# Keys, values and queries as seven half products in a chained PSUM bank, with the residual sums and xn kept in DRAM meanwhile, and the edge table's halves added by GpSimd

## The chip, the cores and the metric

The kernel runs on one core of one Trainium2 chip. The metric is device time in microseconds, the median of the runs; lower is better.

## The reference, cut to what matters

One graph transformer layer over 1250 nodes of 768 features, in float32: a two-layer graph attention (GNN) on 21,250 edges, a linear-attention mixer with an MLP, and a mixture of two of four experts.

```python
xn = layernorm(x)
x  = x + gnn(xn, edges) + mix(xn)
x  = x + ffn(layernorm(x))

# mix(xn)
h = layernorm(xn, ln1_w, ln1_b)
q, k, v = split(h @ qkv_w + qkv_b)            # 768 columns each, 12 heads of 64
q, k = elu(q) + 1, elu(k) + 1
kv = einsum('bhsd,bhse->bhde', k, v)
z  = 1 / einsum('bhsd,bhd->bhs', q, k.sum(-2))
y  = einsum('bhde,bhsd,bhs->bhse', kv, q, z) @ proj_w + proj_b
x1 = xn + y
out = x1 + gelu(layernorm(x1, ln2_w, ln2_b) @ fc1_w + fc1_b) @ fc2_w + fc2_b

# gnn: two attention layers; softmax over the edges into each node
e = leaky_relu(s_src[src] + s_dst[dst]); alpha = softmax of e over the edges of dst
out = segment_sum(alpha * h[src], dst) + bias   # then concat([x, out2]) @ Wu + bu
```

## The kernel before

All matrices lie in SBUF by 128 rows of features or by ten tiles of 125 nodes. Three large tiles last through the kernel: `slot_a` and `slot_x`, each 128 x 7680, and `fT`, the current normalized activations turned (six blocks of 128 features x 1250 nodes). `acc` and `xn` are views of `slot_a` and `slot_x` by ten node tiles: the sum of the residual branches, and the mixer's stream. PSUM has eight banks: two of the pool `p_tp` (`bank4`) and six of the pool `p_mm` (`bank`, one tag, rotating).

The kernel is written with a tile framework. It tracks which tile is read and written, puts in all waits, and orders each engine's instructions at compile time from a list in program order; an instruction that is ready can be placed ahead of earlier ones that are not. Instructions wrapped in `pin` keep program order among themselves on their engine. A tile pool that is closed gives its space to the next one opened at that place.

The stages, in program order:

1. Lines 407 to 509: x is loaded and normalized; `xn` is turned into `fT`; `acc` gets `xn @ Wu` (ps_u). In between, `edge_piece` (line 274) turns the edge list into places in a table of 1250 x 1250 edge multiplicities in DRAM, and GpSimd scatters 170 columns of 125 edges into it, each with an indirect DMA that adds (line 301), alternately into two tables `tabs[0]` and `tabs[1]`, the two halves.
2. Lines 512 to 551: for each of ten tiles, the GNN's first features (ps_g), stored to DRAM from `gt`, a tile of the pool `pk`; `fT` takes the ln1 values meanwhile (`norms`).
3. Lines 564 to 646, in the pool `kvp`: for each tile, keys (ps_k), values (ps_v) and their product (ps_kv). `keys_tile` also adds a bias row `arow` to `acc` and stores it to DRAM (`acc_d`), and adds the projection's bias to `xn`. `wk`, `wv`, `wq`, `wp` are whole weight matrices, loaded on SP's queue.
4. Lines 678 to 720, in the pool `qp`: queries (ps_q) in three column groups of 4, 3 and 3 tiles (`SPLITS`), written to `qT` in `slot_a`. After each group, `ps_z` gets the normalizer and DVE takes its reciprocal and multiplies. `project` (line 688) multiplies kv into the projection's weights ahead of the last group's divisions.
5. Lines 725 to 767: the output projection (ps_p) into `xn`, statistics, and for each tile the ln2 values, turned through PSUM (ps_t) into `fT`.
6. Lines 774 to 1166: the MLP in twelve groups of 256 hidden columns, each in two node ranges (`MIX`). `fc1_unit` (line 781) already computes its product as seven half products: `differences` and `combined` (lines 93 and 103) form sums of quarters of the activations and of the weights, and `product` (line 115) multiplies them, with `more=True` adding onto a bank that a copy has been taken from. `hpool` holds its copies `c1` and `u2`.
   The GNN's attention (`gnn`, line 989) is a generator that yields a cost in us for each step; `spend` (line 1117) adds the cost of each piece of MLP work to a credit, which starts at -20, and takes as many GNN steps as the credit pays for. First of these is `largest` (line 870): for each of ten row blocks the table block is fetched and DVE takes, over four heads, the largest score into each node. Before the fetch, `merged` (line 863) adds the second table to the first in DRAM with an accumulating DMA.
7. Lines 1167 to the end: router, two experts, last layer norm.

## Time and profile before

| | |
|---|---|
| median of 3 runs | 1934.47 us (1929.26 to 1935.96) |
| the profiled execution | 1930.96 us, its span 1929.2 us |
| granted TensorE clock | 0.996 |
| TensorE, DVE, ACT, GpSimd busy | 1896.4, 1330.9, 790.0, 500.7 us |
| scatters into the edge table (line 301) | 170, from 60.4 to 577 us |
| keys and values | 208 to 379 us |
| queries | 377 to 465 us; last divisions to 490 us |
| output projection | 476 to 560 us |
| MLP with the GNN beside it | 560 to 1365 us |
| experts | from 1375 us |

Rows of the trace give start and duration in us, the engine, the line of the kernel, the operation, output `<-` inputs, the shape and how many instructions are merged; in square brackets stands the idle time ahead and what ended it. A float32 matmul of the program is two instructions of the trace. L78 is the line of a helper.

### The profile page before, as it was taken

What the parts mean: (1) busy time and instruction counts of PE and PEld (TensorE: products, weight loads), DVE (VectorE), ACT (ScalarE), POOL (GpSimd) and SP (SyncE); (2) the same over time, 40 slices, a digit from 0 to 9 for tenths busy, and PEclk for the clock granted to TensorE, in tenths of its full rate; (3) what the DMA queues carried; (4) which work ended last, traced back from release to release, by engine and by line L of the source; (5) the groups of instructions that cost most, each with busy time, mean ns of one, the idle gap of its engine ahead of it and who ended that gap; (6) DMA issues with size and microseconds to landing.
All of it is one profiled execution on the core that took longest, in us unless ns stands there. A gap on an engine that the chain in (4) does not pass through costs nothing.

```text
span 1929.2 us, 19359 instructions
## 1 busy us (share of the span) xinstructions
PE 1896.4 (98%) x6978; PEld 1245.5 (65%) x6978; DVE 1330.9 (69%) x2307; ACT 790.0 (41%) x1170; POOL 500.7 (26%) x340
## 2 busy tenths in 40 slices
PE   8989999999999999999999999999999999999998
PEld 7555566545566667877877655666766666666664
DVE  3889533356556976676766967865777777777778
ACT  3223211113131118677874166764374343534330
POOL 2166577688872120111110111100041000000000
PEclk9999999999999999999999999999999999999999
DMA  9844622311119742232442532301485301010023
GB/s 339 272 130 99 198 25 21 69 5 2 2 6 184 142 130 66 74 95 73 113 108 72 142 106 72 104 8 44 129 97 85 85 1 66 0 66 27 31 81 112
DMA packets 180663, 167.78 MB, mean 87 GB/s; under 512 B 108929, under 2 KB 152481, under 8 KB 179287
## 3 DMA queue, kind: packets, MB, share of 16 engines
q0 software_dynamic: 126608, 68.01, 20.4%
q1 hardware_dynamic: 53760, 98.46, 16.0%
q8 instruction: 55, 0.90, 0.2%
q14 instruction: 42, 0.34, 0.1%
q10 hardware_dynamic: 198, 0.07, 0.0%
HBM read 133.94 MB, written 38.20 MB: 89 GB/s over the span
## 4 chain that ended last, share of the span: by engine, by line
PE 70%; issue 9%; POOL 8%; DVE 6%; DMA 5%; ACT 1%; POOLq 0%; DVEq 0%
PE ps_f L830 14%; PE ps_p L78 13%; PE ps_r L78 12%; POOL tab L301 8%; PE ps_o L1006 7%; PE ps_a L119 7%; PE ps_c L119 3%; PE ps_f L1406 3%; PE ps_o L1045 2%; PE ps_k L593 2%; PE ps_v L614 2%; PE ps_d L119 2%; DMA tab<-mult,place_e 1%; PE ps_u L1058 1%; PE ps_g L521 1%
## 5 line engine op out<-in xcount | busy, mean ns | idle before, releaser
L301 POOL DMA_INDIRECT tab<-mult,place_e x170 | 355.0, 2088 | 166.1 <-DMA tab<-mult,place_e 117.5
L830 PE MATMUL ps_f<-w,v 128*125 128x384 f32 x960 | 338.8, 487 | 1.7 <-DVE slot_x L835 1.7
L830 PEld LDWEIGHTS ps_f<-w,v 128*125 128x125 f32 x960 | 177.8, 188 | 110.1 <-issue 11.1
L835 DVE TENSOR_TENSOR slot_x<-ps_f,slot_x 125x384 f32<-125x384 f32 x240 | 131.5, 555 | 56.8 <-PE ps_f L830 52.9
L961 DVE TENSOR_TENSOR wt<-ee 125x375 f32<-125x375 f32 (+1 forms) x180 | 105.9, 590 | 89.7 <-PE ps_o L1006 57.7
L1006 PEld LDWEIGHTS ps_o<-turns,wt 125*125 125x125 f32 x800 | 136.2, 187 | 27.6 <-DVE wt L962 2.2
L1006 PE MATMUL ps_o<-turns,wt 125*125 125x193 f32 x800 | 149.9, 327 | 1.6 <-DVE wt L962 1.6
L956 ACT ACTIVATE ee<-bt,s 125x375 f32<-125x375 f32 (+1 forms) x180 | 114.8, 638 | 88.9 <-DVE wt L961 79.4
L78 PE MATMUL ps_p<-fT,w 128*128 128x312 f32 (+1 forms) x432 | 125.5, 426 | 0.6 <-ACT c L1324 0.6
L962 DVE SCALAR_TENSOR_TENSOR wt<-wt,slot_a 125x375 f32<-125x375 f32 (+1 forms) x180 | 106.0, 591 | 4.9 <-DVE rd L1063 0.2
L78 PEld LDWEIGHTS ps_p<-fT,w 128*128 128x128 f32 x432 | 81.5, 189 | 36.4 <-ACT c L1324 1.1
L78 PE MATMUL ps_r<-w,slot_x 128*125 128x384 f32 x260 | 94.5, 486 | 0.0
L521 PE MATMUL ps_g<-fx,zT 128*125 128x388 f32 x240 | 81.9, 498 | 4.1 <-DVE zT L330 4.1
L119 PE MATMUL ps_a<-fT,w 128*128 128x250 f32 (+1 forms) x288 | 85.0, 426 | 0.7 <-DVE slot_x L736 0.7
L1368 DVE SCALAR_TENSOR_TENSOR slot_a<-ps_r,gate,slot_a 125x384 f32<-125x384 f32 x100 | 60.7, 615 | 33.3 <-PE ps_r L78 33.0
L78 PE MATMUL ps_p<-xt,ws 128*128 128x313 f32 (+1 forms) x288 | 83.5, 425 | 0.0
L495 PE MATMUL ps_u<-wu,fT 128*125 128x384 f32 x240 | 80.0, 490 | 2.4 <-ACT fT L491 2.4
L593 PE MATMUL ps_k<-wk,fT 128*125 128x384 f32 x240 | 80.2, 486 | 0.0
L898 DVE SCALAR_TENSOR_TENSOR slot_a<-turns,s,slot_a 125x1250 f32<-125x1250 f32 x54 | 79.6, 1516 | 0.2
L614 PE MATMUL ps_v<-wv,fT 128*125 128x384 f32 x240 | 79.2, 486 | 0.0
L731 PE MATMUL ps_p<-wq,slot_a 128*125 128x384 f32 x240 | 78.7, 486 | 0.0
L703 PE MATMUL ps_q<-fT,wq 128*128 128x375 f32 (+1 forms) x216 | 76.4, 512 | 0.0
(335 smaller groups left out, 3356.5 us busy)
## 6 DMA issues: line engine op xcount, KB each, us to landing
turns<-g_d POOLq DMA_DIRECT2D x12, 942.4 KB, 13.8
w<-in_L_mix_fc_w_dram SPq DMA_DIRECT2D x12, 768.0 KB
w<-in_L_mix_fc_w_dram SPq DMA_DIRECT2D x24, 384.0 KB
slot_a<-tab POOLq DMA_DIRECT2D x14, 610.4 KB, 6.5
w<-in_L_ffn_w_dram SPq DMA_DIRECT2D x11, 768.0 KB
w<-in_L_ffn_w_dram SPq DMA_DIRECT2D x5, 1536.0 KB
slot_a<-tab POOLq DMA_DIRECT2D x40, 183.1 KB, 3.2
kr<-key_d SPq DMA_DIRECT2D x6, 1062.5 KB
```

The source lines that it names most:

```text
L78: return lambda *args, **kw: pin(getattr(self.engine, name)(*args, **kw))
L119: engine.matmul(ps, wt[:, k, :], x[:, k, :], start=k == 0 and not more, stop=k == n - 1, skip_group_check=more,)
L301: nc.gpsimd.indirect_dma_start(out=tabs[c % 2][:, :], out_offset=bass.IndirectOffsetOnAxis(ap=place[:, c : c + 1], axis=0), in_=mult[:, c ...
L521: nc.tensor.matmul(ps[:TP, :388], zT[:, k, :], fx[:, k, h2 * 388 : (h2 + 1) * 388], start=k == 0, stop=k == KC - 1,)
L593: nc.tensor.matmul(ps[:TP, :w], fT[:, k, tc_], wk[:, k, c0 : c0 + w], start=k == 0, stop=k == KC - 1,)
L614: nc.tensor.matmul(ps[:TP, :w], fT[:, k, tc_], wv[:, k, c0 : c0 + w], start=k == 0, stop=k == KC - 1,)
L830: nc.tensor.matmul(ps, v_of[c][:, f, h, at : at + TP], lasts[g, j][:, f, :], start=f == 0, stop=f == 1,)
L835: nc.vector.tensor_tensor(o, ps, o, ALU.add)
L956: nc.scalar.activation(e[:, 0, :w], bt[:TP, 0, :w], AF.Exp, bias=s[:, 0, h, c : c + 1])
L961: nc.vector.tensor_tensor(wt[:, :w], e[:, 0, :w], e[:, 1, :w], ALU.max)
L962: nc.vector.scalar_tensor_tensor(wt[:, :w], wt[:, :w], 1.0, adj, op0=ALU.min, op1=ALU.mult)
L1006: nc.tensor.matmul(sums[i // 2][:TP, (i % 2) * 193 : (i % 2 + 1) * 193], wt[:, i * TP : (i + 1) * TP], gh[:, c, :], start=c == 0 and i % 2 ...
```

## The change

- Keys and values are computed for pairs of tiles (t, t + 5) by seven products of 3 matmuls each instead of four times 6; queries for six parts (two node ranges, three pairs of column blocks) in the same way. `seven_weights` forms the weight sums, `by_tokens` the activation differences into `xt`, now also a part of `slot_a`. Every chain of a pair uses three banks: `pa`, `pd`, `pc`. Two parts overlap by two products (`overlapped`).
- `acc` is stored whole to `acc_d` on ACT's queue during stage 2 and not added to `arow`; the row goes to DRAM (`brow_d`) and comes in as a row of the GNN's last weights (`wu2x`). `xn` plus the projection's bias is stored to `xn_d` (`leave`), the keys take its place in `slot_x` (`kk`), then the queries (`qT`); it is loaded back into `slot_a` ahead of the output projection. So `acc` and `xn` change places.
- The value bias is added when kv is formed, from the sums of the keys.
- The projection's bias is loaded into the pool `kvp`; `wp` is loaded in `qp`, `hpool` is opened only after `qp` is closed; the pool of `wq` and `wsum` is opened at t == 8 of stage 2.
- The divisions of the first node range stand between query parts, those of the second (12) behind `project`. The output projection takes tiles in the order 0 1 5 6, 2 3 7, 4 8 9.
- `largest` loads both tables' blocks, GpSimd adds them and stores the sum; two buffers take the place of three. The pace is 4.5 for 5.0 and the first credit -27 for -20.

```diff
...
-    qT = slot_a[:, : KC * N].rearrange("p (k n) -> p k n", n=N)
+    qT = slot_x[:, : KC * N].rearrange("p (k n) -> p k n", n=N)
...
+    def seven_weights(w, to):
+        return combined(
+            nc.vector, *(w[:, k : k + 3, c : c + 384] for c in (0, 384) for k in (0, 3)), to
+        )
+    xt = slot_a[:, 2 * D : 2 * D + 9 * HALF].rearrange("p (a b n) -> p a b n", a=3, b=3)
...
+        if t == 1:
+            nc.scalar.dma_start(rows(acc_d, TP), acc)
...
+            nc.sync.dma_start(brow_d, arow[0:1, 0, :])
+        if t == 8:
+            edges.close()
+            mk = mix.enter_context(tc.tile_pool(name="mk", bufs=1, side="right"))
+            wsum = mk.tile([128, 3, 3, 384], F32, name="wsum")
+            wk7 = seven_weights(wk, wsum)
+            by_tokens(nc.vector, xt, 0, TP)
...
-        wp = weights(mk, "wp", a["L0_mix_proj_w"])
+        projb = kvp.tile([TP, D], F32, name="projb")
+        nc.sync.dma_start(projb, bcast(a["L0_mix_proj_b"], TP))
...
+        kk = slot_x[:TP, :].rearrange("p (t f) -> p t f", f=D)
+        def leave(t):
+            nc.vector.tensor_tensor(xn[:, t, :], xn[:, t, :], projb, ALU.add)
+            nc.sync.dma_start(xn_d[t * TP : (t + 1) * TP, :], xn[:, t, :])
...
+            product(nc.tensor, pa, x11, w11)
+            nc.vector.tensor_tensor(c1, pa, b0, ALU.add)
+            yield
+            product(nc.tensor, pd, x21, w12)
+            put(y1[:, :384], pd, c1)
+            yield
+            product(nc.tensor, pa, t2, s2, more=True)
+            nc.vector.tensor_tensor(u2, pa, b0, ALU.add)
+            yield
+            product(nc.tensor, pc, t1, s1)
+            yield
+            product(nc.tensor, pa, t3, s3, more=True)
+            nc.vector.tensor_tensor(u3, pa, b1, ALU.add)
+            put(y2[:, 384:], pc, u3)
+            yield
+            product(nc.tensor, pa, t4, w22, more=True)
+            put(y1[:, 384:], pa, b1)
+            yield
+            product(nc.tensor, pc, x22, s4, more=True)
+            put(y2[:, :384], pc, u2)
...
+        def overlapped(parts, lead=None):
+            for n, (steps, before, done) in enumerate(parts):
+                if n == 0:
+                    before()
+                    take(steps, 2)
+                take(steps, 3)
+                yield
+                if n + 1 < len(parts):
+                    parts[n + 1][1]()
+                    take(parts[n + 1][0], 2)
+                take(steps, 2)
+                done()
...
+        for t in (0, 5, 1, 6):
+            leave(t)
+        parts, sevens = [], {}
+        for t in range(5):
+            def before(t=t):
+                if t == 1:
+                    by_tokens(nc.vector, xt, TP, TP)
+                if t == 2:
+                    by_tokens(nc.vector, xt, 2 * TP, 3 * TP)
+                if t < 3:
+                    leave(t + 2)
+                    leave(t + 7)
+            def done(t=t):
+                if t == 4:
+                    sevens["v"] = seven_weights(wv, wsum)
+            parts.append((keys_pair(t), before, done))
+        late = []
+        for t in range(5):
+            def done(t=t, vs=None):
+                keys_values(t, vs[0])
+                late.append((t + 5, vs[1]))
+            vs = []
+            parts.append((
+                values_pair(t, vs), lambda: None, lambda t=t, vs=vs: done(t, vs)
+            ))
+        for _ in overlapped(parts):
+            while late:
+                keys_values(*late.pop())
+        wq7 = seven_weights(wq, wsum)
...
-    hpool = mlps.enter_context(tc.tile_pool(name="hpool", bufs=1))
...
+        wp = weights(qp, "wp", a["L0_mix_proj_w"])
+        parts = [
+            (queries(i, c), lambda: None, lambda: None) for c in range(2) for i in range(3)
+        ]
...
+        def divided(c, prs):
+            c0, w = MIX[c]
+            for pr in prs:
+                for h in range(2):
+                    ps = bank("ps_z")
+                    o = qT[:, pr, h * HALF + c0 : h * HALF + c0 + w]
+                    nc.tensor.matmul(ps[:, :w], ksum[:, pr, :], o, start=True, stop=True)
+                    rz = qp.tile([128, 375], F32, name="rz", bufs=2)[:, :w]
+                    nc.vector.reciprocal(rz, ps[:, :w])
+                    nc.vector.tensor_tensor(o, o, rz, ALU.mult)
+        for n, _ in enumerate(overlapped(parts)):
+            if n == 1:
+                turned_kv()
+            if n in (7, 9):
+                divided(0, range(3) if n == 7 else range(3, 6))
+        acc, xn = xn, acc
+        project()
+        divided(1, range(6))
...
+        order2 = [(0, 1, 5, 6), (2, 3, 7), (4, 8, 9)]
+        for part in order2:
+            for t in part:
+                nc.sync.dma_start(xn[:, t, :], xn_d[t * TP : (t + 1) * TP, :])
...
+    hpool = mlps.enter_context(tc.tile_pool(name="hpool", bufs=1))
...
+        nc.gpsimd.dma_start(wu2x[96:97, 0, :768], brow_d)
...
-    def merged(c):
-        if c < NT:
-            cs = slice(c * TP, (c + 1) * TP)
-            pin(nc.gpsimd.dma_start(
-                adj_d[cs, :], halves[1][cs, :], accum_op=ALU.add, max_dma_last_dim=N
-            ))
-    def largest(heads, s, b_d, pace, before=lambda c: None, behind=lambda: None):
-        run = slot_a[:TP, : heads * N].rearrange("p (h n) -> p h n", n=N)
-        load = [slot_a[:TP, 5000 + i * N : 5000 + (i + 1) * N] for i in range(2)]
-        load.append(turns[:TP, 0, :N])
+    def largest(heads, s, b_d, pace, merge=False, behind=lambda: None):
+        run = slot_x[:TP, : heads * N].rearrange("p (h n) -> p h n", n=N)
+        own = [slot_x[:TP, 5000 + i * N : 5000 + (i + 1) * N] for i in range(2)]
+        other = [turns[:TP, i, :N] for i in range(2)]
         def fetch(c):
             if c < NT:
-                pin(nc.gpsimd.dma_start(load[c % 3], adj_d[c * TP : (c + 1) * TP, :]))
-        for c in range(3):
-            before(c)
+                cs = slice(c * TP, (c + 1) * TP)
+                pin(nc.gpsimd.dma_start(own[c % 2], adj_d[cs, :]))
+                if merge:
+                    pin(nc.gpsimd.dma_start(other[c % 2], halves[1][cs, :]))
+        def merged(c):
+            if merge and c < NT:
+                pin(nc.gpsimd.tensor_tensor(own[c % 2], own[c % 2], other[c % 2], ALU.add))
+                pin(nc.gpsimd.dma_start(adj_d[c * TP : (c + 1) * TP, :], own[c % 2]))
...
+                if h == heads - 1:
+                    fetch(c + 2)
...
-        yield from largest(4, s1, b1_d, 5.0, merged, lambda: fetch(0))
+        yield from largest(4, s1, b1_d, 4.5, True, lambda: fetch(0))
...
-    credit, cost = -20.0, 0.0
+    credit, cost = -27.0, 0.0
...
```

## The prediction

> **What bounds the kernel now.** I read the page's busy times first, then the chain that ended last, then busy time by stage, and last the order on single engines at the three places that the change touches.
>
> ```profile
> PE 1896.4 (98%) x6978; PEld 1245.5 (65%) x6978; DVE 1330.9 (69%) x2307; ACT 790.0 (41%) x1170; POOL 500.7 (26%) x340
> ```
>
> TensorE leaves 33 us of 1929.2 idle. What a change is worth is therefore its TensorE work, plus new idle time, and at most a few us of old idle time. By stage (columns: TensorE, weight loads, DVE, ACT, POOL, clock, DMA share, GB/s):
>
> ```profile
> 209.00:235.00 26.00, 25.16 (x86) 14.96 (x85) 11.52 (x24) 5.41 (x10) 10.87 (x6) 1.00 0.91 299
> 235.00:300.00 65.00, 65.00 (x227) 39.50 (x226) 18.09 (x32) 8.36 (x16) 47.20 (x23) 1.00 0.24 31
> 600.00:660.00 60.00, 58.28 (x203) 37.60 (x202) 53.98 (x68) 7.75 (x17) 13.02 (x14) 1.00 1.09 197
> ```
>
> In the keys and values (from 208 us) TensorE is full and DVE mostly idle. In the column maxima of the edge table (600 to 700) DVE is nearly full too. At the start of the keys, the chain:
>
> ```profile
> 209.08 12.23 DMA g_d<-gt
> ...
> 221.43 0.57 DVE kk L599 x2
> ...
> 234.84 5.16 PE ps_k L593 x16
> ```
>
> The last row prices a product: 5.16/16 = 0.3225 us an instruction, two instructions to a 384-column matmul. The first two show a wait: the keys' first DVE write, into the pool opened after `pk` closed, waits until the last store out of `pk` (gt) has landed. It costs TensorE 0.8 us, because six banks let it run on:
>
> ```profile
> 208.37 15.64 PE L593 MATMUL ps_k<-wk,fT 128*125 128x384 f32 x48
> 223.85 7.90 PE L614 MATMUL ps_v<-wv,fT 128*125 128x384 f32 x24
> ```
>
> **The products.** The skill's page "Trainium Kernel Development and Optimization", Performance Expectations, calls matmul busy time a bad measure and weight-load share a good one. That share is 65% here; by it there would be slack for an eighth fewer matmuls to vanish in. But the row above shows full-speed instructions back to back, 0.3225 us against 0.19 us for a weight load, so removed matmuls are time. Keys: 120 matmuls become 5 pairs x 7 x 3 = 105; 30 instructions x 0.3225 = 9.7 us. Values the same. Queries: 45,000 columns become 39,375, two passes at 0.84 ns a column (0.3225/384): 9.4 us. Together -28.8 us.
>
> **The keys' start.** One pair uses three banks, and its third product adds onto the first one's bank, so it waits until `c1` has copied it. `c1` lies in the same new pool as `kk` did, so it can't be written before 221.4 + 0.6 = 222.0. TensorE has the first two products until 212.3 and the fourth (1.9 us) if it is issued early. Idle: 9.7 or 7.8 us. Also new on that stage: four sums of the keys' weights (128x1152; the 128x1125 row of L97 takes 1.32) and four differences, 7.5 us of DVE after 206.7, done by 215 and so hidden by the 222. Then `leave`: the projection's bias now lands in that pool too, so its load, issued on SP after wv and wq, waits for 221.4 and lands at perhaps 227; what stands behind the first `leave` on DVE (u2, for the fifth product) then waits, and so do the `put`s, as the keys overwrite xn once it is stored. If other pairs' products are pulled ahead, 2 us; if a `leave` stands ahead of u2, 16. I take 10, since DVE in the trace took kk before the second tile's ready sums: the compiled order did not foresee the long wait.
>
> **The divisions.** Now:
>
> ```profile
> 464.75 7.90 PE L693 MATMUL ps_pm<-wp,kvb 128*128 128x384 f32 x24
> 472.49 3.95 PE L717 MATMUL ps_z<-slot_a,ksum 128*128 128x375 f32 x12
> 476.27 24.03 PE L731 MATMUL ps_p<-wq,slot_a 128*125 128x384 f32 x74
> ```
> ```profile
> 473.32 4.87 DVE L719 RECIPROCAL rz<-ps_z 128x375 f32<-128x375 f32 x2 [6.75 <-PE ps_z L717]
> 478.11 0.94 DVE L720 TENSOR_TENSOR slot_a<-slot_a,rz 128x375 f32<-128x375 f32 x2
> ```
>
> Six z products fill six banks and the output projection follows at once. DVE needs 2.44 + 0.47 = 2.91 us for each. After the change twelve of this size stand there. The seventh waits for the first reciprocal, the projection's first bank for the seventh: 0.6 + 2.44 + 6 x 2.91 = 20.5 us, in which TensorE has 12 x 0.66 = 7.9 us of work. Idle 12.6 us. Below: 0, if z products slip into gaps of the queries. I take 12.6, as those stages have no gaps to slip into. The other twelve (250 columns, 1.63 + 0.4 us) go between query parts of 13 us: 0 to 8, take 2.
>
> **The MLP's start.** `hpool` is now opened after `qp` closes, so c1 of the first fc1 unit waits for qp's last reader, the transposes of the last z2. That such a pool waits whole is seen in the waits of the SP queue, for the load of av2, the first tile behind qp:
>
> ```profile
> SPq L841 <- PE ps_t L758: 84.0, 1, 84.0
> ```
> ```profile
> 573.45 0.93 PE L758 MATMUL ps_t<-ident,z 125*128 125x125 f32 x6
> ```
>
> The last projection is evicted at 560.0, the last transpose ends at 574.3. About 3 us of that is ACT doing fc1's work (a table load of 1.28, gelus, copies), which now comes later: 11.5 us. TensorE has three products of 250 columns (1.27 each) and three tiles' transposes of 0.8: 6.2. Idle 5.3 to 8; I take 6.
>
> **The edge table.** Scatters are paced by POOL and the table's own DMAs, so they end where they do now:
>
> ```profile
> 572.43 1.99 POOL L301 DMA_INDIRECT tab<-mult,place_e  x1 [1.88 <-DMA tab<-mult,place_e]
> 577.66 4.64 POOL L866 DMA_DIRECT2D tab<-tab  x3 [3.24 <-DMA tab<-mult,place_e]
> ...
> 588.28 0.57 POOL L879 DMA_DIRECT2D slot_a<-tab  x1 [5.98 <-DVE slot_x L835]
> ```
> ```profile
> 603.84 0.81 DVE L894 TENSOR_SCALAR turns<-slot_a 125x1250 f32<-125x1250 f32 x1 [4.45 <-DMA slot_a<-tab]
> ```
>
> Accumulating in DRAM and loading back takes 26 us; two loads (0.55 each to issue, 6.5 to land) and an add take about 11. The trace has no POOL add. Its nearest row is a 128x1250 POOL memset, 1.14 us, the low end; the skill's "GPSIMD Engine Reference", 3.1, has 4497 ns for 2048 elements, so 2.7 us as an estimate, which I take, as an add reads two inputs. The same page (4.1) speaks against the move: elementwise work belongs on VectorE. There ten adds would cost about 15 us (1.5 each by L898's row) in a window where DVE is 54/60 busy; on POOL, 13/60 busy, 27 us lie free. So the measured loads decide for POOL. The table is ready near 590, and the maxima are asked for some 50 us after the MLP starts, so the present DVE wait and its 1.7 us of TensorE idle go. Against that, two buffers replace three: from the end of column c to the table of c+2 is 1.1 + 6.5 + 2.7 = 10.3 us, where pace 4.5 leaves about 9.4; eight waits near 0.9 us, mostly under three ps_f banks: +2. In the second layer 7.1 against 5.4: +1. Net +1.3; ends -2 and +25.
>
> **The rest.** The ten sums `acc + arow` (0.95 each) go: nothing, DVE is idle there. acc's store, 3.75 MB, moves to ACT's queue near 135 us, beside key loads on SP and the scatters; ACT feeds zT to TensorE, which waited 4.1 us there already: 0 to 8, take 1. The weight sums of values and queries, 5.4 us each, must follow the last use of `wsum`: 0 to 6, take 1, as the next part's first two products cover them. xn's reloads on SP (3 MB) land under the projection of kv and the divisions; wp's load has the 66 us of queries; brow_d is one row on POOL: nothing.
>
> **Sum.** -28.8 + 10 + 12.6 + 2 + 6 + 1.3 + 1 + 1 = +5.1 us on the profiled execution's 1930.96, so 1936.1. Its time lies 3.5 us under the median of the runs, so about 1940 there. A measurement tells about 0.3%, 5.8 us, from no change.
>
> **Rivals.**
> A, the forecast (0.45): three waits eat the gain; 1930 to 1948, a little over half of it slower by more than 0.3%.
> B, faster (0.33): the three waits are half covered, because the compiled order pulls later pairs' products and z products into them: -14 us, and the small terms vanish: about 1918. For it: TensorE's order already fills gaps (ps_k between ps_kv). Against: banks, which an early product also needs.
> C, slower (0.22): the maxima wait for the table. It decides from landing times: at 6.5 us the cycle per column is (10.3 + 9.2)/2 = 9.8 us and costs almost nothing; at 10 us, (13.8 + 9.2)/2 = 11.5, 2 us over, nine times: +18 on DVE, of which TensorE loses some 13: 1953. For it: DMA share 1.09 in that window, g_d's loads land in 13.8. Against: the DRAM accumulation leaves, which moved more bytes.
> That the products are not fewer is excluded by the diff.
>
> Range 1915 to 1957, which takes in B's middle and most of C. Faster by over 0.3%: B and a sliver, 0.34; within: 0.22 from A; slower: the rest of A and C, 0.44.
>
> **What would show it.** Matmuls of keys and values 210 instructions each at 0.32 us; idle TensorE of 8 us or more near 212 with c1 waiting for g_d's store; some 12 us before the output projection, with reciprocals running; 6 us at the MLP's start behind ps_t; first maxima not waiting for the table. I am wrong if the first and second gaps are under 3 us (then B) or if L894's line waits for loads or POOL several us per column (then C).

## The result

The changed kernel takes 1995.7 us (median of four, 1994.3 to 1998.8) where the kernel before takes 1934.2 beside it: a ratio of 1.0324 (95% interval 1.0302 to 1.0347). It is slower by 62 us. The forecast was 1940, its range ended at 1957, so it had the side of the likeliest case and missed the size by 56 us.

The page of the changed kernel, busy times (span 1992.5 us):

```profile
PE 1902.4 (95%) x6966; PEld 1254.6 (63%) x6966; DVE 1362.9 (68%) x2375; ACT 816.5 (41%) x1224; POOL 527.1 (26%) x361
```

TensorE is busy 6 us longer than in the kernel before, although products were taken out, and its idle time grew from 33 to 90 us. A busy time that does not fall with the work means that some of the instructions ran slower. The same page, the granted clock of TensorE in 40 slices of 50 us:

```profile
PEclk9998899998989999999999999999999999999999
```

Four slices show it below nine tenths. By stretches (columns: TensorE, weight loads, DVE, ACT, POOL, each with its instructions; clock, DMA share, GB/s):

```profile
124.00:180.00 56.00, 39.76 (x112) 21.41 (x111) 33.06 (x60) 12.93 (x32) 22.17 (x10) 0.88 0.54 171
...
240.00:300.00 60.00, 54.82 (x151) 30.05 (x150) 33.87 (x59) 17.00 (x32) 23.82 (x13) 0.90 0.34 97
480.00:560.00 80.00, 72.87 (x228) 40.93 (x229) 51.85 (x79) 11.99 (x23) 66.80 (x34) 0.89 0.19 5
560.00:600.00 40.00, 32.89 (x119) 21.59 (x118) 20.85 (x41) 12.26 (x24) 31.82 (x17) 0.87 0.19 7
660.00:727.00 67.00, 56.62 (x175) 33.95 (x174) 52.62 (x59) 7.16 (x15) 24.13 (x20) 0.95 0.58 162
```

In each, TensorE is idle for some us and its clock is low as well. I cut the trace at four instructions that both kernels have: the first product of the keys, the last transpose of the key-value product (`ps_kvT`), the first product of the MLP, the first sum of the attention. In the changed kernel 11 us of query products stand ahead of that transpose, in the kernel before 2; they count in the second column. Stretches in us; "repaired" is the last run below:

| | to the keys | keys, values | to the MLP | to the first attention sum | rest |
|---|---|---|---|---|---|
| before | 208.4 | 172.0 | 179.7 | 167.4 | 1201.9 |
| after | 223.8 | 179.6 | 176.3 | 206.7 | 1206.1 |
| after, repaired | 205.6 | 161.0 | 159.8 | 213.0 | 1154.5 |

After the first attention sum only 4 us were lost. (In the repaired run the maxima start later on purpose, so work moves from the last column to the one before it.) Taking each form of instruction (operation and shape) at its median time, I split every stretch into work, idle time and the remainder, which I count as work at a lower clock. Over the whole kernel the work fell by 23 us, idle time rose by 57 and the slow remainder by 29: 63 us, as the spans have it (1929.2 to 1992.5).

**To the keys: +15.** VectorE, ScalarE, then TensorE, of the changed kernel:

```profile
155.27 0.93 DVE L474 TENSOR_TENSOR zT<-fT,ps_r 128x750 f32<-128x750 f32 x1 [15.71 <-issue]
155.30 0.06 DVE L526 MEMSET gt<- 125x4 f32 x1
```
```profile
171.38 0.48 ACT L535 COPY gt<-ps_g 125x384 f32<-125x384 f32 x1 [13.09 <-DMA g_d<-gt]
```
```profile
158.87 10.33 PE L530 MATMUL ps_g<-fx,zT 128*125 128x388 f32 x24 [10.24 <-DVE zT L332]
169.03 0.38 PE L466 MATMUL ps_r<-ident,rst 125*128 125x125 f32 x2
172.45 9.80 PE L530 MATMUL ps_g<-fx,zT 128*125 128x388 f32 x23 [3.04 <-DVE zT L332]
```

VectorE stands 15.7 us with no releaser that the profile can name. The work that follows at once is a memset of `gt`, so I take it that it stood for a free buffer of `gt`, that is for a store of g1. ScalarE's later copy into `gt`, held up for 13.1 us, names such a store as what it waited for. The queues from 142 to 148 us, when only acc's store and g1's stores are under way (packets, MB, share of 16 engines; q10 is ScalarE's queue with acc's store, q1 SP's):

```profile
q10 hardware_dynamic: 194, 0.60, 24.5%
q1 hardware_dynamic: 194, 0.15, 7.7%
```

From 130 to 172 us acc's store of 3.75 MB moves at about 97 GB/s and never fills more than a quarter of the engines; g1's stores trickle beside it. The two queues have the same number of packets, 194, but acc's are rows of 3 KB and g1's pieces of 772 bytes. Together they fill 32.2%, about five engines of 16.

**Keys and values: work for 10 us less, 7.6 us more time.** TensorE and VectorE, changed kernel:

```profile
239.49 4.20 PE L121 MATMUL ps_ka<-wsum,slot_a 128*125 128x384 f32 x6 [6.50 <-DVE c L630]
...
245.70 2.10 PE L121 MATMUL ps_ka<-wk,fT 128*125 128x384 f32 x6
...
257.19 4.20 PE L121 MATMUL ps_ka<-wk,fT 128*125 128x384 f32 x6 [4.22 <-DVE slot_x L623]
```
```profile
238.87 1.02 DVE L630 TENSOR_TENSOR c<-ps_ka,kvb 125x384 f32<-125x384 f32 x2 [6.97 <-DMA g_d<-gt]
...
256.57 0.56 DVE L623 TENSOR_TENSOR slot_x<-ps_kd,c 125x384 f32<-125x384 f32 x1 [1.68 <-DMA xn_d<-slot_x]
```

The two waits of the prediction are there: `c1` for the last g1 store, `slot_x` for the store of xn. Behind each, six instructions take 4.20 us, where six take 2.10 between them: half speed.

**To the MLP: 19 us less work, 3.4 us less time.** The divisions, TensorE:

```profile
472.72 4.58 PE L876 MATMUL ps_z<-slot_x,ksum 128*128 128x375 f32 x14
478.47 0.90 PE L876 MATMUL ps_z<-slot_x,ksum 128*128 128x375 f32 x2 [1.17 <-DVE rz L878]
481.74 1.62 PE L876 MATMUL ps_z<-slot_x,ksum 128*128 128x375 f32 x2 [2.37 <-DVE rz L878]
...
493.00 3.56 PE L906 MATMUL ps_p<-wq,slot_x 128*125 128x384 f32 x5 [1.65 <-DVE rz L878]
```

From the first of these products, at 472.72, to the projection are 20.3 us; 8.3 of them are idle.

**From the MLP's start to the first attention sum: +39.** From its first product to the first of fc2 are 20.3 us with 6.5 idle (in the kernel before 14.8 us with none). The larger part is the loop of the first maxima. GpSimd, changed kernel:

```profile
704.88 0.67 POOL L1060 DMA_DIRECT2D tab<-slot_x  x1 [0.30 <-POOL slot_x L1059]
705.54 0.54 POOL L1053 DMA_DIRECT2D slot_x<-tab  x1
706.08 0.52 POOL L1055 DMA_DIRECT2D turns<-tab  x1
714.84 2.83 POOL L1059 TENSOR_TENSOR slot_x<-slot_x,turns 125x1250 f32<-125x1250 f32 x1 [8.24 <-DMA turns<-tab]
718.39 0.53 POOL L1060 DMA_DIRECT2D tab<-slot_x  x1 [0.72 <-POOL slot_x L1059]
```

One column in series: store, two fetches, a landing of 8.2 us, the add of 2.83. VectorE starts its columns at the pace of that loop:

```profile
704.62 0.81 DVE L1072 TENSOR_SCALAR turns<-slot_x 125x1250 f32<-125x1250 f32 x1 [4.43 <-POOL slot_x L1059]
717.70 0.81 DVE L1072 TENSOR_SCALAR turns<-slot_x 125x1250 f32<-125x1250 f32 x1 [4.50 <-POOL slot_x L1059]
731.71 0.81 DVE L1072 TENSOR_SCALAR turns<-slot_x 125x1250 f32<-125x1250 f32 x1 [5.15 <-POOL slot_x L1059]
```

From first to last start it is 12.2 us a column (635.25 to 745.38, nine steps), 13 to 14 in the second half, against 9.1 before (603.84 to 685.88).

### The profile page after: what moved, and what is told of

The parts are those of the page before. It is cut to its first block, busy times and chain, and to the rows that moved or that the text cites. A ratio compares the mean times of both kernels' runs of the same rounds, so it can differ in the third digit from the quotient of the medians.

```text
span 1992.5 us, 19523 instructions
## 1 busy us (share of the span) xinstructions
PE 1902.4 (95%) x6966; PEld 1254.6 (63%) x6966; DVE 1362.9 (68%) x2375; ACT 816.5 (41%) x1224; POOL 527.1 (26%) x361
## 4 chain that ended last, share of the span: by engine, by line
PE 82%; DMA 7%; DVE 6%; ACT 2%; issue 1%; POOL 1%; ACTq 0%; DVEq 0%; POOLq 0%; SPq 0%
PE ps_p L80 13%; PE ps_f L1007 13%; PE ps_r L80 11%; PE ps_o L1186 7%; PE ps_a L121 6%; PE ps_p L906 4%; PE ps_u L497 4%; PE ps_c L121 3%; PE ps_f L1586 3%; DMA turns<-tab 3%; PE ps_o L1225 2%; PE ps_g L530 2%; DMA g_d<-gt 2%; PE ps_va L121 2%; PE ps_qa L121 2%; PE ps_d L121 2%
## 5 line engine op out<-in xcount | busy, mean ns | idle before, releaser
L1007 PE MATMUL ps_f<-w,v 128*125 128x384 f32 x960 | 344.8, 492 | 15.7 <-DVE slot_a L1012 15.5
L1012 DVE TENSOR_TENSOR slot_a<-ps_f,slot_a 125x384 f32<-125x384 f32 x240 | 132.1, 554 | 65.2 <-PE ps_f L1007 61.6
L1142 DVE SCALAR_TENSOR_TENSOR wt<-wt,slot_x 125x375 f32<-125x375 f32 (+1 forms) x180 | 105.9, 591 | 4.6
L530 PE MATMUL ps_g<-fx,zT 128*125 128x388 f32 x240 | 84.5, 510 | 16.0 <-DVE zT L332 15.9
L80 PE MATMUL ps_r<-w,slot_a 128*125 128x384 f32 x260 | 94.5, 486 | 0.0
L1076 DVE SCALAR_TENSOR_TENSOR slot_x<-turns,s,slot_x 125x1250 f32<-125x1250 f32 x54 | 84.2, 1601 | 0.1
L1548 DVE SCALAR_TENSOR_TENSOR slot_x<-ps_r,gate,slot_x 125x384 f32<-125x384 f32 x100 | 60.7, 615 | 33.3 <-PE ps_r L80 33.0
L906 PE MATMUL ps_p<-wq,slot_x 128*125 128x384 f32 x240 | 81.3, 498 | 1.7 <-DVE rz L878 1.7
L956 ACT ACTIVATE v<-v,par 128x250 f32<-128x250 f32 (+1 forms) x72 | 40.1, 557 | 91.6 <-DVE v L989 31.9
L530 PEld LDWEIGHTS ps_g<-fx,zT 128*125 128x125 f32 x240 | 45.7, 195 | 50.5 <-DVE zT L332 15.2
L1139 ACT ACTIVATE ee<-bt,s1l 125x375 f32<-125x375 f32 (+1 forms) x120 | 75.7, 631 | 0.1
```

Of the source, the lines that this page charges most:

```text
L80: return lambda *args, **kw: pin(getattr(self.engine, name)(*args, **kw))
L530: nc.tensor.matmul(ps[:TP, :388], zT[:, k, :], fx[:, k, h2 * 388 : (h2 + 1) * 388], start=k == 0, stop=k == KC - 1,)
L906: nc.tensor.matmul(ps[:TP, :w], qT[:, k, t * TP : (t + 1) * TP], pm[:, k, c0 : c0 + w], start=k == 0, stop=k == KC - 1,)
L1007: nc.tensor.matmul(ps, v_of[c][:, f, h, at : at + TP], lasts[g, j][:, f, :], start=f == 0, stop=f == 1,)
L1012: nc.vector.tensor_tensor(o, ps, o, ALU.add)
L1142: nc.vector.scalar_tensor_tensor(wt[:, :w], wt[:, :w], 1.0, adj, op0=ALU.min, op1=ALU.mult)
```

## The experiments

Theory A: the saving is there, and separate waits in five places eat it, each made dearer by a low clock behind it. Its rivals: bytes or clock as such; one cause early that only shows later; or VectorE simply has too little room. Ratios are to the kernel before, run beside; the changed kernel's is 1.0324. Two ratios can differ by some 0.003 (6 us) by chance, so I read the stretch as well. The planner is `spend` with its credit and the pace. The edits are shown shortened.

**The maxima as before** (slots stay exchanged).

```
-    own[c % 2] += other[c % 2] on GpSimd; store; fetch(c + 2)
+    dma_start(adj_d[cs], halves[1][cs], accum_op=add); three loads
-    largest(4, s1, b1_d, 4.5, True, ...); credit -27
+    largest(4, s1, b1_d, 5.0, True, ...); credit -20
```

> The first column maxima get their table as in the kernel before: DRAM-side adds of the second half onto the first, three load buffers, pace 5.0 and credit -20; the slots stay exchanged as in the changed kernel. Theory A (GpSimd's one loop of fetch, landing 8.3 us, add 2.8 us and store sets 13.3 us a column and starves VectorE and then TensorE's output tiles): the stretch from the first hidden product to the first attention sum falls from 207 us to about 172, the column period to about 9.5 us, and the time by 30 to 37 us to about 1962. Rival B (the later end of the scatters, 606 instead of 577 us, holds the maxima whatever form the adds have, because they stand behind it): the stretch stays above 195 us and the time above 1985. Rival C (the stretch is lost to the lower clock of that stage alone): no change within 5 us.

Ratio 1.0177 (1.0152 to 1.0202): 28 us back. The stretch fell to 175.2 us, the period to 9.1 us. The last of its scatters starts at 602 us, as late as the changed kernel's (603.6), so Rival B falls; this one part is nearly half of the loss.

**Only the planner's numbers** (credit -20, pace 5.0; GpSimd's adds stay).

> The changed kernel with nothing but the planner's numbers of the kernel before: credit -20 instead of -27 and pace 5.0 instead of 4.5 for the first maxima; GpSimd's adds stay. It tells how much of the 28 us that the maxima as before took back are the pace's. Theory A (GpSimd's loop sets 13.3 us a column, longer than either pace): the column period stays at 13 us, the stretch to the first attention sum at 200 us or more, the time within 5 us of the changed kernel's ratio 1.032. Rival B (the pace of 4.5 is what makes TensorE wait for VectorE): the time falls by 12 us or more.

Ratio 1.0294 (1.0269 to 1.032), the stretch 201.4, the period 12.2. Some 6 us of the 28 are the pace's and the credit's; the loop has the rest.

**GpSimd's adds with two columns on their way.**

```
-    adj, far = own[c % 2], other[c % 2]
+    adj, far = own[c % 2], (a place of its own)
-    merged(c + 1) ahead of the column; fetch(c + 2) after its last head
+    fetch(c + 2); merged(c + 1) after the first head
```

> GpSimd still adds the halves, but VectorE writes its penalty (far) into a place of its own, so that the fetches of column c+2 are issued right after VectorE's first work on column c and two columns are on their way while the third is worked on. All else is the changed kernel. Theory A (the loop of one landing, one add and one store in series, 8.3 + 2.8 + 1.7 us, is what costs, not GpSimd's add as such): the column period falls from 13.3 to 9.5 to 10 us, the stretch from the first hidden product to the first attention sum from 207 to about 172 us, and the time by 28 to 36 us. Rival B (GpSimd's add, at 2.8 us and in the way of VectorE, or the loads' bytes cost by themselves): the period stays at 12 us or more and the gain is under 12 us.

Ratio 1.0227 (1.021 to 1.0244): 19 us back, stretch 190.9, period 10.9 (633.57 to 731.78). GpSimd in this run:

```profile
646.58 0.52 POOL L1057 DMA_DIRECT2D turns<-tab  x1
647.11 2.84 POOL L1061 TENSOR_TENSOR slot_x<-slot_x,turns 125x1250 f32<-125x1250 f32 x1
650.25 0.53 POOL L1062 DMA_DIRECT2D tab<-slot_x  x1 [0.30 <-POOL slot_x L1061]
656.82 0.54 POOL L1055 DMA_DIRECT2D slot_x<-tab  x1 [6.05 <-DMA tab<-slot_x]
```

The add no longer waits for a landing, but the next fetch stands 6 us for the store of the buffer that it overwrites. The series is what costs, not the add. The gain lies between the two theories: I had overlooked the store, so two buffers of the first half are still one too few.

**acc's store in two**, rows 0 to 112 and 112 to 125.

```
-    nc.scalar.dma_start(rows(acc_d, TP), acc)
+    for p0, p1 in ((0, 112), (112, TP)):
+        nc.scalar.dma_start(rows(acc_d, TP)[p0:p1], acc[p0:p1])
```

> The store of acc is issued as two transfers, rows 0 to 112 and rows 112 to 125, as the loads of x are; all else is the changed kernel. Theory A (the one store over 125 rows occupies about 4 of the 16 DMA engines for 45 us, 0.24 of their time, and the stores of g1 queue on those engines, so that gt's buffers come free late): the store's busy share rises to 0.8 or more and it is over in about 12 us, the two long waits of VectorE and ScalarE for g1's store (15.7 and 13.1 us) fall under 4 us, the stretch before the keys shrinks from 103 us to 88, and the time falls by 12 to 17 us to about 1981. Rival B (the bytes themselves delay g1's stores, however they are spread): the stretch stays at 100 us or more and the time within 4 us of 1996.

Ratio 1.0294 (1.0271 to 1.0317); the keys start at 216.3, 7.5 us sooner. The store now takes 57% of the engines and is over in 17 us, but one wait of VectorE stays at 11.9 us. Half right. What it left, from 148 to 153 us, with q10 empty and g1's stores alone on q1:

```profile
q1 hardware_dynamic: 585, 0.45, 31.4%
```

That is about 90 GB/s, on the share of engines that both stores had together before, so g1's own stores are slow too.

**acc's store tile by tile** over the steps t = 0 to 6, in the same two parts, with ScalarE's order held.

> acc leaves tile by tile over the steps t = 0 to 6 of the loop, each tile in rows 0 to 112 and 112 to 125, all on ScalarE's queue, instead of in one store at t = 1. The store in two parts took 17 us on the DMA engines and gained 7 of the 15 us. Theory A (the rest of the loss is the g1 stores that stand beside the big store): the stretch before the keys falls from 103 to 90 us or less and the time by 10 to 15 us against the changed kernel. Rival B (the rest lies in VectorE's sums of weights and tokens at the end of the loop, which the kernel before did not have): the stretch stays at 95 us or more and the gain at 8 us or less.

Ratio 1.0287 (1.0264 to 1.031); keys at 214.2, 9.6 us sooner. From the first g1 product to the keys it is 92.6 us, where the changed kernel has 103 and the kernel before 87.7: between the two theories.

**g1's stores in two; acc's stays whole.**

```
-        nc.sync.dma_start(g1_d[:, t * TP : (t + 1) * TP, :]..., gt)
+        for p0, p1 in ((0, 112), (112, TP)):
+            nc.sync.dma_start(g1_d[:, t * TP + p0 : t * TP + p1, :]..., gt[p0:p1])
```

> The changed kernel with only g1's stores cut into rows 0 to 112 and 112 to 125; acc's one big store over 125 rows stays as it is. Theory A (the number of DMA engines counts: acc's store sits on the few engines that a transfer of 125 rows gets, and g1's stores of 125 rows get the same few, while 112 rows get others too; the Trainium skill, DMA: Bandwidth & Descriptors, on how many engines a transfer takes, has the largest divisor up to 16 of the row count, which for 125 is 5 and for 112 is 16, on the lowest-numbered engines): the share of g1 that lies on free engines lands soon, but each store still has some rows on the busy ones, so the waits for g1's store shorten from 29 us to under 15, the stretch before the keys falls from 103 to 92 to 97 us, and the time by 5 to 10 us. Rival B (the order of the two queues or the bytes decide, not the engines): no change within 4 us.

Ratio 1.025 (1.0227 to 1.0273): 14 us back, more than either cut of acc's store, and more than Theory A had. The stretch from the first g1 product to the keys fell from 103 to 90.4 us. The queues from 142 to 148 us again:

```profile
q10 hardware_dynamic: 206, 0.63, 26.0%
q1 hardware_dynamic: 482, 0.35, 23.0%
```

acc's store is as slow as it was, and g1's stores move more than twice the bytes past it. So not bytes and not the queue's order: what counts is how many engines a store gets. The Trainium skill ("DMA: Bandwidth & Descriptors", the paragraph on how many engines, under why a DMA increments its semaphore by 16) has the rule: such a transfer is cut over the largest number of engines, up to 16, that divides the outer dimension of both its sides, and it takes the lowest-numbered ones. For 125 rows that is 5 of 16, a share of at most 31%, for 112 it is 16. The trace agrees: 31.4% for g1's stores alone and 32.2% for both stores at once, 57% for acc's store once cut. The trace does not number the engines, but a sum of 32.2% fits two stores on the same five. The scatters gained too: their last starts at 594.1 us instead of 603.6.

**Other places for the keys, first trial**: the bias loaded ahead of the loop over g1 and four tiles of xn stored inside it, `c1` and `kex` in a pool opened before it.

> The projection's bias is loaded before the loop over the first layer's tiles, the first four tiles of xn leave within that loop (t = 4 to 7), and c1 and one kex buffer stand in a place of their own instead of the closed pool of gt; u2 stays. Theory A (the keys start late since c1 waits for the last g1 store and slot_x for the bias row's load and then xn's store): the gaps of 6.5 and 4.2 us, and the half-clock stretches behind them, go; keys and values together lose under 8 us instead of 19, and the time falls by 9 to 14 us to about 1984. Rival B (VectorE itself is behind in that stretch with sums of weights, tokens and biases): the gaps move to other waits of TensorE for VectorE, and the time falls by under 4 us.

Ratio 1.0474 (1.0443 to 1.0505): 29 us slower. Keys and values took 168.8 us, 11 less, as Theory A said, but two new waits cost more; the largest in the loop. SP's queue, then TensorE's wait:

```profile
143.76 0.27 SPq L524 DMA_DIRECT2D xn_d<-slot_x  x1
178.46 0.27 SPq L897 DMA_DIRECT2D slot_a<-xn_d  x1
...
179.21 0.30 SPq L548 DMA_DIRECT2D g_d<-gt  x1
```
```profile
PE ps_g L538 <- DVE zT L332: 37.4, 3, 35.0
```

A tile of xn that had left early could be loaded back early, so the compiled order put that load (L897) ahead on SP's queue; it had to wait until acc's store had read `slot_a`, and a g1 store stood behind it.

**Second trial, with that order held**: the bias loaded at t = 2, the stores and loads of SP's queue pinned; xn leaves where it did in the changed kernel.

> The bias of the projection is loaded at t = 2 into a place that is open before the loop, c1 and one kex buffer stand there too, and the order of the g1 stores, of the stores of xn and of its loads is held as in the program (the earlier trial of this let loads of xn run ahead on the queue). Theory A (c1 behind the last g1 store, and slot_x behind the bias row and xn's store, cost what the keys lose): keys and values lose under 9 us instead of 19, the stretch before them stays near 103, and the time falls by 8 to 12 us against the changed kernel. Rival B (VectorE is late in that stretch by itself): the gaps stay at other waits for VectorE and the gain is under 4 us.

Ratio 1.0303 (1.0278 to 1.0328). Keys and values 171.9 us, 7.7 less: idle plus slow time 11 us instead of 19. The largest waits left are 2.9 us for `u2`, which still stood behind g1's store, and 2.7 for `slot_x`. The start of the keys, 2.4 us later, took some back, so the whole gained only 4 us: Theory A holds for the stretch, but not for the time.

**The divisions spread**: first node range after query parts 1 to 3, second after parts 5 and 6, the last two blocks beside the projection's first tiles.

```
-    if n in (7, 9): divided(0, ...)
+    if n in (3, 5, 7): divided(0, ...)
+    if n in (9, 11): divided(1, ...)
-    divided(1, range(6))
```

> The divisions are spread: those of the first node range after query parts 1 to 3, those of the second after parts 5 and 6, and its last two feature blocks between the first tiles of the output projection; the same arithmetic. Theory A (the 20.3 us between the first late z product and the output projection are twelve reciprocals of 375 columns in VectorE's order, and VectorE has room for them beside the queries): queries to projection lose 2 us instead of 10.5, and the time falls by 8 to 12 us to about 1986. Rival B (VectorE is full beside the queries too, so the reciprocals only hold TensorE at other places): the time falls by under 3 us.

Ratio 1.0282 (1.0261 to 1.0303): 8 us. To the MLP it is 160.4 us, 16 less, and TensorE's row shows the products inside the queries with no wait:

```profile
452.96 2.68 PE L876 MATMUL ps_z<-slot_x,ksum 128*128 128x375 f32 x8
455.48 2.06 PE L121 MATMUL ps_qa<-slot_a,wsum 128*128 128x375 f32 x6
...
461.15 0.79 PE L876 MATMUL ps_z<-slot_x,ksum 128*128 128x375 f32 x2
```

The clock came back as well. Of the 16 us the maxima took back 4.

**Maxima as before, divisions spread, and z2 in its own place** (so that `hpool` waits only for readers long done).

> Three repairs together: the first maxima as before (which alone took back 28 us), the divisions spread over the query parts (which alone took back 8 us, 16 in its stage of which 4 were lost again in the maxima), and z2 in a place of its own so that the MLP's c1, u2 and v need not wait for the last normalized tile. Theory A (the costs add, since they lie in different stages): time 1995.7 - 28 - 12 to 16 - 3 to 6, about 1949, ratio 1.005 to 1.011. Rival B (the maxima's end is held by the scatters at 604 us or by VectorE's room in the MLP, so that an earlier MLP start is given back there): 1957 or more.

Ratio 1.0172 (1.0153 to 1.019), nothing beyond the maxima alone: Rival B. The MLP's start is mended (6.4 us from its first product to the first of fc2, none idle, against 20.3 and 6.5), and the MLP begins at 564.0. But VectorE's wait in that stretch is

```profile
DVE turns L1077 <- DMA slot_x<-tab: 31.5, 1, 31.5
```

The last scatter begins at 607.6. An earlier MLP asks for the table earlier; it does not come earlier.

**All repairs, credit -32**: acc by tiles, the keys' places with `u2` too and four tiles of xn stored in steps 6 to 9, divisions, z2; once with GpSimd's adds and three buffers of the first half, once with the maxima as before.

> All repairs on the changed kernel: acc's store spread by tiles; the bias, c1, kex and u2 in places that do not wait for the last g1 store, the first four tiles of xn leaving in steps t = 6 to 9; divisions spread over the query parts; z2 in a place of its own; GpSimd's adds with three buffers of the first half, two of the second and the penalty apart; credit -32, since the MLP would now start near 545 us while the scatters end near 595. Theory A (the loss was these five waits and the half clock behind each; the products' saving stands): stretches before the keys 91, keys and values 167, to the MLP 160, to the first attention sum 172: the time falls to about 1915, ratio 0.988 to 0.995. Rival B (an earlier MLP is given back at the maxima, whose table comes no earlier than about 612 us): the last stretch stays at 185 or more and the time at 1928 or more, ratio 0.997 or above.

> The same, but with the maxima as in the kernel before (adds by DMA in DRAM, three buffers, pace 5.0), credit -32. Theory A: as the run with GpSimd's adds, but the table is ready later (three adds in DRAM and a fetch stood between the last scatter at 602 us and the first maximum at 632 us when the maxima alone were put back), so VectorE stands at the first maximum some 10 to 20 us and the time is 5 to 15 us above the run with GpSimd's adds. Rival B (GpSimd's add hinders VectorE or the transfers): it is the faster of the two.

Ratios 1.0016 (1.0004 to 1.0029) and 0.9994 (0.9981 to 1.0007). In the first Rival B holds. In the second the keys begin at 205.6 and the MLP at 532.3 us, 27.7 sooner than in the kernel before: the promised saving, and the whole no faster. It goes here, in TensorE's and in VectorE's rows of the second run:

```profile
617.31 2.92 PE L1013 MATMUL ps_f<-w,v 128*125 128x384 f32 x4 [27.99 <-DVE slot_a L1018]
```
```profile
615.80 0.99 DVE L1079 TENSOR_SCALAR turns<-slot_x 125x1250 f32<-125x1250 f32 x1 [32.29 <-DMA slot_x<-tab]
```

The first maximum stands in VectorE's order for the table, the MLP's sums behind it, and TensorE's output tiles behind those. Contrary to my expectation the DMA adds were no slower than GpSimd's.

**Only the start of the maxima moved**: credit -60 with the maxima as before, credit -46 with GpSimd's adds.

> As the run of all repairs with the maxima as before, whose MLP started at 532 us (28 us sooner than in the kernel before) but whose TensorE then stood 28 us in one wait for VectorE's first maximum, which stood for the table (last scatter at 587 us). Only the credit is changed, from -32 to -60: the maxima start 28 us of matmuls later. Theory A (the saving of the products is there, and is lost only in that one wait): the wait is under 3 us, and the time falls by 20 to 28 us to 1903 to 1912, ratio 0.985 to 0.990. Rival B (maxima moved later leave the attention less of the MLP's matmuls to run beside, so the time is given back at the attention's sums or at the end): 1922 or more.

> As the run of all repairs with GpSimd's adds, where TensorE stood 12.6 us in one wait for the first maximum and 25.8 us in all in that stretch; only the credit is changed, from -32 to -46. Theory A: the one wait goes and the time falls by 10 to 14 us to about 1924; the other 13 us of idle and the half clock stay, since GpSimd's column period of 10 us or more is unchanged. Rival B: no gain, as the period alone sets the end of the maxima.

Ratios 0.9909 (0.9892 to 0.9925) and 0.9969 (0.9953 to 0.9984): both faster than the kernel before, the first a little less than Theory A had. In the first, 8.7 us of the one wait remain; in the second 15.9 us of idle time remain in the stretch.

**The best of these with g1's stores in two and credit -72.**

> The best run so far (all repairs, maxima as before, credit -60), with credit -72 and g1's stores cut into rows 0 to 112 and 112 to 125. In that run TensorE still stood 8.7 us in one wait for the first maximum. Theory A: that wait goes, and the time falls by 6 to 10 us to about 1905, ratio 0.984 to 0.988; the keys' one wait of 3.8 us for u2 stays. Rival B (the attention by then has too little of the MLP beside it): no gain or a loss of up to 10 us.

Ratio 0.9824 (0.9807 to 0.9842), 1896.1 us, 33 us faster than the kernel before. The two changes were not run apart here. Its page, and the stretches that were worst:

```profile
PE 1866.9 (99%) x6966; PEld 1241.9 (66%) x6966; DVE 1355.1 (72%) x2375; ACT 800.2 (42%) x1213; POOL 506.5 (27%) x341
```
```profile
240.00:300.00 60.00, 60.00 (x203) 35.99 (x203) 23.30 (x42) 15.59 (x31) 46.77 (x23) 1.00 0.21 22
480.00:560.00 80.00, 79.12 (x293) 49.10 (x293) 39.49 (x85) 27.50 (x56) 67.71 (x34) 1.00 0.20 9
...
660.00:727.00 67.00, 67.00 (x258) 45.17 (x257) 59.51 (x85) 8.64 (x18) 10.41 (x14) 1.00 0.47 116
```

TensorE is busy 29.5 us less than in the kernel before (1896.4 to 1866.9), full in nearly every stretch, and the clock is 1.00. The last scatter begins at 570.0 us, where all repairs without the cut of g1's stores had it at 587 to 592.

## Why the prediction failed

In the prediction's own terms: the sum of its waits was 34 us of idle time, and idle time rose by 57; it put nothing for the clock, which took 29. The sizes given below for the store and the maxima contain their share of slow work, so they cannot be added to it.

**The products (-28.8): right.** At full speed the products of keys, values and queries take 201.9 us instead of 230.6 (their instructions counted, each form at its median), 28.7 less, and the best run's TensorE is 29.5 us less busy. That the removed matmuls are time, and not slack that a share of weight loads suggests, is confirmed.

**The keys' start (+10): right in the waits and in their sum.** The two gaps are 6.5 and 4.2 us, 10.7 together. The first was put at 7.8 to 9.7, so it was shorter and the second longer than reckoned; that the sum fits so well is in part luck. The stage lost another 6.4 us to slow work.

**The divisions (+12.6): right.** 20.5 us were reckoned from the first product to the projection, 20.3 measured: VectorE's row of reciprocals sets it. Of the 12.6 us of idle time 8.3 are idle and the rest went into slow products. The spread gave back 16 us of the stretch. **The other divisions (+2)** and **the sums of weights (+1)** show no wait above 1 us.

**The MLP's start (+6): right**, 6.5 us idle.

**acc's store (+1, bounds 0 to 8): wrong, 15 us.** The step that failed is "ACT feeds zT to TensorE, which waited 4.1 us there already: 0 to 8": it looked at the issuing queue only. The cost is on the DMA engines, where a store over 125 rows sits on a few engines that g1's stores need as well, 42 us long. The runs that cut either store show it: 7 to 13 us of the stretch from g1 to the keys came back.

**The maxima (+1.3, upper end 25): wrong, the largest miss.** About 22 us: 28 in the run with the loop undone, less some 6 for the pace and the credit. The step that failed is the sum "from the end of column c to the table of c+2 is 1.1 + 6.5 + 2.7 = 10.3 us", and with it Rival C's half of (10.3 + 9.2). It lets two columns overlap. In the program's held order on GpSimd, `merged(c + 1)` stands ahead of `fetch(c + 2)` and `merged(c + 2)` behind it, so one landing lies in each column: 8.2 + 2.8 + 0.3 + 0.7 + 1.1 = 13.1 us, and 13 to 14 are measured. The landing (6.5 taken, 8.0 to 8.9 measured in the second half) accounts for 2 us of it, the add (2.7 estimated, 2.83 measured) for none. Rival C named the right place with the wrong loop, and the sign that it gave came: VectorE waits 4.4 to 5.3 us a column for GpSimd at the end.

**The scatters "end where they do now": wrong.** 603.6 instead of 572.4 us. GpSimd's waits between 240 and 300 us, kernel before, then changed kernel:

```profile
POOL tab L301 <- DMA tab<-mult,place_e: 9.4, 4, 3.9
```
```profile
POOL tab L303 <- DMA tab<-mult,place_e: 39.9, 10, 9.1
```

Each scatter waits for earlier ones to land. In that window 13 scatters start instead of 22, while SP's queue, with the stores of xn and loads, moves 5.8 MB instead of 1.3; that its transfers hold the scatters up is argued, not shown. In the changed kernel the delay cost little, as its MLP began late too; it is what took the saving away once the other waits were gone. With all repairs the window has 23 scatters again, and what stays late comes from before 240 us: 36 have started by then with credit -60, 44 when g1's stores are cut as well (40 in the kernel before and in the changed one). The last then begins at 570.0 instead of 591.6. These two runs differ in g1's stores and in the credit alone, and the credit acts only from the MLP on, so g1's stores on few engines held scatters up.

**The clock: not priced, 29 us.** Every wait was put in at its idle time. Waits come with work at half speed: 4.20 us for six instructions instead of 2.10 behind the gaps of 6.5 and 4.2 us. The Trainium skill ("TensorE: Matmul & The Clock Gate", part 1) says that the clock halves after an idle window of about 3.4 us and returns after as much work. Both gaps fit it. At the divisions no gap was above 2.4 us, yet products between them took 1.62 us for two instead of 0.79 as in the run with the divisions spread; so here several short gaps in a row were enough. No run takes the clock apart from the waits: it is seen with each and went with each.

## What to carry to other kernels

Write a loop of fetch, work and store in the order in which its engine will issue it, and count how many landings lie in one turn: two buffers do not make two fetches in flight if the next fetch stands behind a wait for the last. Cut a transfer of 125 rows (112 and 13) before spreading it or moving it, above all if others of that shape wait for their buffers. And when time is won upstream, look for the next thing that is asked for earlier and does not come earlier; here one number of the planner held back 16 us (0.9994 to 0.9909).

## What was unexpected of the hardware

Many short waits cost more clock here than one long one. In the changed kernel 30.3 us of idle time between the MLP's start and the first attention sum came with 15.1 us of slow work; in the run with all repairs and credit -32, 30.7 us of idle time in the same stretch, 28.0 of it in one piece, came with 3.3 us. And stores of 377 KB over 125 rows in pieces of 772 bytes are slow by themselves: with the other queue empty, SP's queue moved them at about 90 GB/s on 31.4% of the engines. Beside a store with rows of 3 KB, g1's got the same number of packets, 194 each in 6 us, and so a fifth of the bytes (0.15 of 0.75 MB).
